# Value projection by rows, with the attention windows gathered through DRAM

## The chip, the cores and the metric

The kernel runs on one core of one Trainium2 chip. The metric is the device time of one launch in microseconds (us). A core has TensorE (PE, matrix products), VectorE (DVE), ScalarE (ACT) and GpSimd (POOL), each with its own instruction queue that is worked off in order, and DMA engines that move data between SBUF (on-chip memory, 128 partitions), PSUM (where PE writes) and DRAM. In this kernel nearly all DMAs are issued from the queue of SyncE (SP). Engines wait for each other through semaphores. A difference under 0.2% of the time is about what a measurement of this kernel can't tell from none.

## The reference, cut to what matters

The input `x` has shape (2, 128, 256, 256), all in float32. The layer is halo attention followed by a mixture of experts, each with a normalization in front and a residual add behind.

```python
qkv = einsum('bchw,oc->bohw', ln(x), W_qkv)          # 128 channels -> q, k, v of 128 each
q = 8x8 windows of q; k, v = 12x12 windows around the same places (overlapping, zero-padded)
attn = q @ k.T * SCALE + rel_pos + FIXED_MASK        # -inf where row or column offset is of the wrong parity
x = x + W_out @ (softmax(attn) @ v)
t = tokens of x
x = x + sum over the 2 best of 8 experts: gate_e * (ln(t) @ expert_w[e] + expert_b[e])
```

The fixed mask leaves, for a query, only keys whose row and column have one parity. So the image falls into four planes (row parity by column parity) that don't see each other. In one plane a window of queries is 4 by 4, and its window of keys is 6 rows by 10 columns for two neighbouring windows taken together (60 keys, `NK`).

## The kernel before, in words

The image is cut into 64 strips of 8 rows (2 images, 32 strips each), each strip into its 4 planes: 256 steps of the main loop (line 779 on), one plane of one strip each, and 7 more that finish the experts. In a plane a strip has 4 rows of 128 queries, and 6 rows of keys (`KR`), two of which it shares with its neighbours; 128 columns of queries make 16 pairs of windows (`NP`), in two halves of 8 (`HP`).

The work inside the loop is issued in the order in which it is written: `tc.manual_schedule` covers PE, DVE, ACT, POOL and SP, so what stands first in the loop's body stands first in each queue. In step n four things are interleaved:

- attention of plane n: `scores` (L448 and L465, products of 32x64 tiles), the exponential L473 on ACT, `attend` (L486 sums, L496 values), normalization by DVE (L506 to L516), `out_project` (L524 on PE, L529 on DVE);
- the projections of plane n+1: `project`, a generator that the loop advances five times. It makes the values in two parts (`values`, L369 on PE and L376 on ACT), the relative position terms `pu` (L384, then L386, L349 and L354 on DVE), the keys `pk` (L396, copied by ACT L407 and L414 into the windowed layout `kcol`) and the queries `pq` (L418, L420);
- the experts of a row pair: `Experts.times` multiplies by the gate (L677, six times on DVE, twice on POOL), `product` is L686 on PE, eight per step, `end` is L692 on DVE;
- the normalization and routing of the next row pairs: statistics by PE (L554), `rstd` (L228 to L235 on DVE, with two activations L232 and L233 on ACT between), `route` (L587 to L619), `spread` (L625), which sends gates and the reciprocal deviations through a small DRAM tile `gd` and back, spread over all partitions: one load `rb` for the attention's normalization (L637), used by POOL's L272 in the same step to make a row of `xn`, and nine loads `sb` and `gb` (L666, L661) for the experts, used one step later.

[...] `columns` (L331) therefore has POOL copy the rows of `xn` that are new in a strip into `xcol`, window by window, and `values` then multiplies 16 blocks of two windows' keys: 8 products of 128x128 a step, `vv` with keys on the partitions. Keys of a block are ordered by ring row (`place`, a row's place modulo 6), then by column. The rows of keys that a strip shares with the one before stay in `xcol` and `kcol`, which are rings.

PSUM tiles of `mm_tile` come from one pool of three buffers in turn; a product that takes a buffer waits until the reader of the tile three before it is done. In a step that order is `pvv`, `pu`, `pk`, `pq`, `plt`, `plg`, `pvv`, `po`.

Of the kernel before, what the change touches and what calls it, by code (L numbers as in the profile page):

```python
# [11 lines left out]
F32 = mybir.dt.float32  # L12
AF = mybir.ActivationFunctionType
ALU = mybir.AluOpType
# [3 lines left out]
P = 128  # L18
# [33 lines left out]
def kernel(  # L52
# [42 lines left out]
    def ctile(shape, name):  # L95
        return const.tile(shape, F32, tag=name, name=name)
# [101 lines left out]
    xn, xcol, kcol = [], [], []  # L198
    for i in range(2):
        xn.append(ctile([P, 2, 2, KR, PC + 2], f"xn{i}"))  # L200
        nc.gpsimd.memset(xn[i][:, :, :, :, 0 : PC + 2 : PC + 1], 0.0)
    for i in range(4):
        xcol.append(ctile([P, HP, 2, SLOT], f"xcol{i}"))
        kcol.append(ctile([P, NP, SLOT], f"kcol{i}"))
        nc.gpsimd.memset(xcol[i][:, :, :, NK:], 0.0)
        nc.gpsimd.memset(kcol[i][:, :, NK:], 0.0)
        nc.gpsimd.memset(kcol[i][:, 0, 0:NK:KC], 0.0)
        nc.gpsimd.memset(kcol[i][:, NP - 1, KC - 1 : NK : KC], 0.0)


    auT = []
# [6 lines left out]
    def rstd(p4, k0, k1, name):  # L218

        u, r = (
            small.tile([P, 2, NT], F32, tag=v, name=f"{v}_{name}")[:, k0:k1] for v in ("u", "r")
        )
        mean, sq = (
            p4[:, :, E + 2 * k0 + j : E + 2 * k1 : 2].rearrange("p t k -> p k t") for j in range(2)
        )
        nc.vector.tensor_copy(r, mean)  # L228
        nc.vector.tensor_tensor(u, r, r, ALU.mult)
        nc.vector.scalar_tensor_tensor(u, u, -1.0, sq, ALU.mult, ALU.add)  # L230
        nc.vector.scalar_tensor_tensor(u, u, 0.0, epsc[:, k0:k1], ALU.max, ALU.add)
        nc.scalar.activation(r, u, AF.Ln, scale=4.0)  # L232
        nc.scalar.activation(r, r, AF.Exp, scale=-0.5)  # L233
        nc.vector.scalar_tensor_tensor(u, u, -4.0, r, ALU.mult, ALU.mult)
# [16 lines left out]
    def place(i, k):  # L251

        return (PR * strips[i][1] + k) % KR
# [69 lines left out]
            ln1(i, k, pb, nc.vector)  # L323
        yield

    def columns(n):

        i, pl = divmod(n, 4)
        for k, at, m in runs(i, ln_rows(i)):
            for half in range(2):  # L330
                nc.gpsimd.tensor_copy(  # L331
                    xcol[pl][:, :, half, at * KC : (at + m) * KC].rearrange(
                        "p t (r c) -> p t r c", c=KC
                    ),
                    windows(xn[i % 2][:, pl // 2, pl % 2, k : k + m], half * HP, HP),
                )
        for k, s in ((0, 0), (KR - 1, NS - 1)):
            if strips[i][1] == s:
                c0 = place(i, k) * KC
                nc.gpsimd.memset(xcol[pl][:, :, :, c0 : c0 + KC], 0.0)  # L340
                nc.gpsimd.memset(kcol[pl][:, :, c0 : c0 + KC], 0.0)

    def shift(uT, n, state):

# [12 lines left out]
    def project(n, state):  # L357

        i, pl = divmod(n, 4)
        xp = xn[i % 2][:, pl // 2, pl % 2]  # L360
        inner = xp[:, 1 : 1 + PR, 1 : PC + 1]
        xl, kk = xcol[pl], kcol[pl]

        vv = work.tile([P, HP, P], F32, tag="vv", name=f"vv{n}")

        def values(t0):
            pv = mm_tile(f"pvv{n}_{t0}")
            for t in range(4):
                nc.tensor.matmul(  # L369
                    pv[:, t * P : (t + 1) * P],  # L370
                    lhsT=xl[:, t0 + t].rearrange("p a k -> p (a k)"),
                    rhs=wv,
                    start=True,
                    stop=True,
                )
            nc.scalar.copy(vv[:, t0 : t0 + 4, :].rearrange("p t c -> p (t c)"), pv)  # L376

        values(0)
        yield

        pu = mm_tile(f"pu{n}")
        nc.tensor.matmul(pu, lhsT=wrel, rhs=inner, start=True, stop=True)  # L384
        uT = work.tile([P, PR, 4, 32], F32, tag="uT", name=f"uT{n}", bufs=1)
        nc.vector.transpose(uT, pu.rearrange("p (a m s) -> p a s m", a=PR, s=4))  # L386
        state["shift"] = lambda: shift(uT, n, state)
        yield

        rows = list(ln_rows(i))  # L390
        for part in (rows[-4:], rows[:-4]):
            if not part:
                continue
            pk = mm_tile(f"pk{n}_{part[0]}")
            m = len(part)
            nc.tensor.matmul(  # L396
                pk[:, : m * PC],
                lhsT=wk,
                rhs=xp[:, part[0] : part[0] + m, 1 : PC + 1],
                start=True,  # L400
                stop=True,
            )
            pk3 = pk[:, : m * PC].rearrange("p (r c) -> p r c", r=m)
            for k, at, m in runs(i, part):
                new = pk3[:, k - part[0] : k - part[0] + m]
                places = kk[:, :, at * KC : (at + m) * KC].rearrange("p t (r c) -> p t r c", c=KC)
# [3 lines left out]
                for j, step in enumerate(((NP - 1) * SLOT - 1, PC - KC + 1)):  # L410
# [12 lines left out]
        yield  # L423

        values(4)
        state.update(qs=qs, kk=kk, vv=vv)
        yield

    def windows(rows, n0, count):
# [192 lines left out]
    def spread(f, c, g, nm):  # L622

        gT = small.tile([P, 2, 32], F32, tag="gT", name=f"gT{nm}")
        nc.vector.transpose(  # L625
            gT.rearrange("p k i -> p (k i)"), g.rearrange("p k b j -> p (k b j)")
        )
        gd = dram.tile([2 * E * NT, P], F32, tag="gd", name=f"gd{nm}")

        to = gd.rearrange("(k j t) (b i) -> k (t b) j i", k=2, j=E, i=32)  # L630
        for k in (1, 0):
            if k or f:
                nc.sync.dma_start(to[k], gT[:, k])
        rb = None
        if c:
            rb = gates.tile([P, NT * P], F32, tag="rb", name=f"rb{nm}", bufs=2)
            nc.sync.dma_start(rb, to_all(gd, E + 1))  # L637
        return gd, rb

    def to_all(gd, j):  # L640

# [103 lines left out]
            next(part)  # L745
    if len(strips) > 1:
        halo(1)
    columns(0)
    states = {0: {}}
    for _ in project(0, states[0]):  # L750
        pass
    states[0]["shift"]()
    if n_planes > 1:
        columns(1)

# [22 lines left out]
    with tc.manual_schedule(engines={ET.PE, ET.DVE, ET.Activation, ET.Pool, ET.SP}):  # L778
        for n in range(n_planes + 7):
# [89 lines left out]
def shape_constants():  # L869

    keys = np.zeros((HEADS, 32, 3, 2, KR, KC), np.float32)
    for turn in range(3):
        for r in range(KR):
            keys[:, r, turn, :, (r + 2 * turn) % KR, :] = 1.0
    for w in range(2):
        for c in range(KC):
            keys[:, KR + c - 4 * w if 0 <= c - 4 * w < 6 else KR + 6, :, w, :, c] = 1.0
    keys = np.pad(keys.reshape(P, 3, 2, NK), ((0, 0), (0, 0), (0, 0), (0, SLOT - NK)))
# [47 lines left out]
```

The softmax here doesn't subtract the row's maximum and nothing guards it: scores larger than these inputs give would overflow.

## Time and profile before

| what | value |
|---|---|
| median of 3 runs | 4483.97 us (4482.62 to 4489.09) |
| profiled execution, span | 4480.1 us |
| PE busy | 4422.6 us (99%) |
| DVE busy | 3996.2 us (89%) |
| ACT busy | 1467.7 us (33%) |
| POOL busy | 1317.7 us (29%) |
| DMA engines, share of the span, SP's queue | 58.3%, 813.46 MB |
| granted TensorE clock, mean | 0.997 |

The profiled execution is one launch of its own; its span, from the first to the last instruction, is 3.9 us under the median of the runs. A step of the loop takes 17.17 us in the trace in the mean of the long middle part. PE's records overlap[...]; the time that a product takes from PE is therefore read from start to start, not from its own length. A float32 product shows as two matmul records. "Idle before" in a group's line is time in which that engine did nothing just ahead of those instructions.

### The profile page before, as it was taken

The numbers are of one execution on the slowest core, as the hardware profiler recorded it, in microseconds if no ns is written. First come the engines' busy times: TensorE is split into PE (matmuls) and PEld (weight loads), VectorE is DVE, ScalarE is ACT, GpSimd is POOL, SyncE is SP. The second block draws the span as 40 slices with busy tenths as digits, with TensorE's granted clock in tenths as the row PEclk, the third lists the DMA queues.
The fourth block names the chain that finished last, engine by engine and source line by source line (L and its number), as shares of the span: only waits on it lengthen the run. The fifth ranks groups of instructions, "written<-read, shape, count | busy, mean of one in ns | idle before, by whom it ended". The sixth has DMA issues, their size and how long they took to land. (4 is left out here: it accounts for less than half of the span.)

```text
span 4480.1 us, 224632 instructions
## 1 busy us (share of the span) xinstructions
PE 4422.6 (99%) x96321; PEld 2683.3 (60%) x96321; DVE 3996.2 (89%) x11850; ACT 1467.7 (33%) x4022; POOL 1317.7 (29%) x1815
## 2 busy tenths in 40 slices
PE   7999999999999999999999999999999999999997
PEld 5666666666666666666666666666666666666653
DVE  5899999999899999998989999999999999989887
ACT  3333333333333333333333333333333333333321
POOL 1232323232323233232323232323232323232321
PEclk9999999999999999999999999999999999999999
DMA  2565666566656666666666566666665666566655
GB/s 83 174 191 185 192 185 192 186 191 185 193 184 192 185 191 187 189 188 188 189 187 189 187 190 185 193 183 193 184 193 185 192 185 192 186 191 186 190 164 186
DMA packets 519284, 828.12 MB, mean 185 GB/s; under 512 B 124186, under 2 KB 125850, under 8 KB 518298
## 3 DMA queue, kind: packets, MB, share of 16 engines
q1 hardware_dynamic: 517568, 813.46, 58.3%
q8 instruction: 769, 12.60, 1.1%
q14 instruction: 217, 1.78, 0.2%
q10 hardware_dynamic: 730, 0.29, 0.0%
HBM read 737.95 MB, written 75.56 MB: 182 GB/s over the span
## 5 line engine op out<-in xcount | busy, mean ns | idle before, releaser
L686 PE MATMUL acc<-xe,ew 128*128 128x512 f32 x4096 | 1889.0, 594 | 19.6 <-DVE gb L660 18.8
L686 PEld LDWEIGHTS acc<-xe,ew 128*128 128x128 f32 x4096 | 758.8, 190 | 885.7 <-issue 861.8
L677 DVE TENSOR_TENSOR xe<-xs,gb 128x512 f32<-128x512 f32 x1536 | 950.9, 687 | 10.2 <-PE acc L686 0.7
L681 POOL COPY last<-xe 128x1 f32<-128x1 f32 x256 | 47.9, 187 | 3060.8 <-DVE gb L660 3054.6
L376 ACT COPY vv<-pvv 128x512 f32<-128x512 f32 x512 | 299.8, 586 | 1395.7 <-PE pvv L369 1379.6
L677 POOL TENSOR_TENSOR xe<-xs,gb 128x512 f32<-128x512 f32 x512 | 650.8, 1272 | 5.9 <-PE att L496 2.5
L369 PE MATMUL pvv<-wt,xcol 128*128 128x128 f32 x4096 | 594.3, 288 | 2.5 <-POOL xcol L331 1.5
L369 PEld LDWEIGHTS pvv<-wt,xcol 128*128 128x128 f32 x4096 | 496.4, 191 | 64.8 <-issue 51.8
L272 POOL TENSOR_TENSOR xn<-xt,rb 128x512 f32<-128x512 f32 x249 | 375.0, 1506 | 66.5 <-DMA rb<-gd 55.9
L465 PE MATMUL att<-qs,kcol 32*64 32x32 f32 x32768 | 392.4, 226 | 0.8 <-issue 0.7
L465 PEld LDWEIGHTS att<-qs,kcol 32*64 32x64 f32 x32768 | 391.0, 130 | 1.0 <-issue 1.0
L496 PEld LDWEIGHTS att<-pT,vv 64*32 64x32 f32 x32768 | 348.0, 105 | 39.4 <-issue 2.5
L496 PE MATMUL att<-pT,vv 64*32 64x32 f32 x32768 | 343.2, 200 | 2.3 <-issue 2.3
L473 ACT ACTIVATE pT<-att 128x1024 f32<-128x1024 f32 x256 | 261.9, 1023 | 243.1 <-PE att L465 239.7
L548 ACT ACTIVATE sq<-xt 128x512 f32<-128x512 f32 x505 | 292.7, 631 | 0.0
L354 DVE STREAM_TRANSPOSE au<-auT 128x512 f32<-128x512 f32 x256 | 269.2, 1052 | 9.0
L524 PE MATMUL po<-o,wt 128*128 128x512 f32 x512 | 262.0, 593 | 6.1 <-DVE o L516 3.2
L384 PE MATMUL pu<-xn,wrel 128*128 128x512 f32 x512 | 262.5, 594 | 0.0
L407 ACT COPY kcol<-pk 128x560 f32<-128x560 f32 (+2 forms) x344 | 174.1, 506 | 268.2 <-PE pk L396 265.3
L418 PE MATMUL pq<-xn,wt 128*128 128x512 f32 x512 | 262.0, 593 | 0.0
L396 PE MATMUL pk<-xn,wt 128*128 128x512 f32 (+2 forms) x528 | 261.0, 578 | 0.0
L386 DVE STREAM_TRANSPOSE uT<-pu 128x512 f32<-128x512 f32 x256 | 182.8, 714 | 78.0 <-PE pu L384 77.0
(2697 smaller groups left out, 5243.8 us busy)
## 6 DMA issues: line engine op xcount, KB each, us to landing
gb<-gd SPq DMA_DIRECT2D x2048, 256.0 KB, 4.0
xt<-in_x_dram SPq DMA_DIRECT2D x256, 256.0 KB, 4.9
sb<-gd SPq DMA_DIRECT2D x256, 256.0 KB, 3.5
out_dram<-xt SPq DMA_DIRECT2D x256, 256.0 KB, 4.2
rb<-gd SPq DMA_DIRECT2D x249, 256.0 KB, 3.3
gd<-gT SPq DMA_DIRECT2D x516, 16.0 KB, 3.0
ew<-in_L_ffn_expert_w_dram SPq DMA_DIRECT2D x1, 512.0 KB, 5.0
eb<-in_L_ffn_expert_b_dram SPq DMA_DIRECT2D x1, 512.0 KB, 5.7
```

The source lines that it names most:

```text
L272: eng.tensor_tensor(xn[i % 2][:, :, :, k, 1 : PC + 1], ln1_src(i, k).rearrange("p (y j x) -> p y x j", y=2, x=2), rb.rearrange("p (y j x) ...
L354: nc.vector.transpose(au.rearrange("p m a s -> p a s m"), auT[n % 2])
L369: nc.tensor.matmul(pv[:, t * P : (t + 1) * P], lhsT=xl[:, t0 + t].rearrange("p a k -> p (a k)"), rhs=wv, start=True, stop=True,)
L376: nc.scalar.copy(vv[:, t0 : t0 + 4, :].rearrange("p t c -> p (t c)"), pv)
L384: nc.tensor.matmul(pu, lhsT=wrel, rhs=inner, start=True, stop=True)
L418: nc.tensor.matmul(pq, lhsT=wq, rhs=inner, start=True, stop=True)
L465: nc.tensor.matmul(sc[rows, h, 32 * t : 32 * t + 32], lhsT=kk[hp, half * HP + t, :], rhs=qs[hp, m0 : m0 + 2].rearrange("p m a s -> p (m a ...
L496: nc.tensor.matmul(av[hp, half, 32 * t : 32 * t + 32], lhsT=vv[rows, t, hp], rhs=pT[rows, h, 32 * t : 32 * t + 32], start=True, stop=True,)
L524: nc.tensor.matmul(po, lhsT=wo, rhs=state["o"].rearrange("p f z -> p (f z)"), start=True, stop=True)
L548: nc.scalar.activation(sq, src, AF.Square)
L677: eng.tensor_tensor(self.xe[e], self.xs, self.gb.pop(e), ALU.mult)
L686: nc.tensor.matmul(self.acc, lhsT=ew[:, e, :], rhs=self.xe.pop(e), start=(e == 0), stop=not self.xe)
```

## The change

- The values are no longer computed from windowed blocks. `value_rows` multiplies each new row of a plane by the value weights: a row's 128 columns are the stationary operand, so the product has columns on the partitions and the 128 value channels along the free dimension. For most strips that is 4 products of 128x128 a step into one PSUM tile, and one ACT copy into `vr`; strips at an image's top and bottom have 5 and 3 rows.
- `send_values` stores `vr` in DRAM, in a ring `vrows` for each plane, by column and then by ring row: one store of 256 KB, two where the new rows wrap around the ring (one strip in three).
- `take_values` loads the windows from there: two loads a step, one for each half of the windows, of 60 keys by 8 windows by 512 bytes, into `vwin`, which takes the place of `vv`.
- A block's keys are now ordered by column, then by ring row, in `kcol` (L434 and L441 on ACT) and in the constant `c_keys` too.
- `xcol` and POOL's copies into it are gone; `borders` keeps the clearing of rows outside the image.
- In the loop, `send_values` stands between the stores of `gd` and the load of `rb`; `take_values` stands behind the load of `sb`, ahead of the first `gb`. `project` now begins with `pu`, then the value products, and its fifth part issues nothing.
- In `rstd`, the square is now taken as r times `mean`, where `mean` is still the PSUM tile, and not as r times r.

```diff
-        nc.vector.tensor_tensor(u, r, r, ALU.mult)
+        nc.vector.tensor_tensor(u, r, mean, ALU.mult)
...
-    def columns(n):
+    def borders(n):
...
+    def value_rows(n):
+        i, pl = divmod(n, 4)
+        xp = xn[i % 2][:, pl // 2, pl % 2]
+        rows, sent = list(ln_rows(i)), []
+        for part in (rows[-4:], rows[:-4]):
...
+            pv = mm_tile(f"pv{n}_{part[0]}")
+            for j, k in enumerate(part):
+                nc.tensor.matmul(
+                    pv[:, j * P : (j + 1) * P],
+                    lhsT=xp[:, k, 1 : PC + 1],
+                    rhs=wv,
...
+            vr = work.tile([P, 4, P], F32, tag="vr", name=f"vr{n}_{part[0]}")
+            nc.scalar.copy(
+                vr[:, 0:m].rearrange("p r c -> p (r c)"), pv[:, : m * P]
+            )
...
+    def send_values(n, sent):
+        i, pl = divmod(n, 4)
+        for part, vr in sent:
+            for k, at, m in runs(i, part):
+                nc.sync.dma_start(
+                    vrows[pl][1 : PC + 1, at : at + m, :],
+                    vr[:, k - part[0] : k - part[0] + m],
+                )
+
+    def take_values(n):
+        for half in range(2):
+            src = vrows[n % 4][half * HP * 8 : half * HP * 8 + KC].rearrange("c r d -> (c r) d")
+            src = src.unsqueeze(1)
+            dims = [list(d) for d in src.ap]
+            dims[1] = [8 * KR * P, HP]
+            nc.sync.dma_start(
+                vwin[n % 2][half * SLOT : half * SLOT + NK],
+                bass.AP(src.tensor, src.offset, dims),
+            )
...
-        values(0)
-        yield
...
         nc.tensor.matmul(pu, lhsT=wrel, rhs=inner, start=True, stop=True)
+        state["sent"] = value_rows(n)
+        yield
+
...
-        values(4)
-        state.update(qs=qs, kk=kk, vv=vv)
+        state.update(qs=qs, kk=kk, vv=vwin[n % 2])
         yield
...
-                gd, rb1 = spread(f, c, made[0], f"_{n}")
-                row = (*c, rb1) if c else None
+                gd = spread(f, c, made[0], f"_{n}")
                 new = Experts(*f, gd) if f else new
+            if n + 1 < n_planes:
+                send_values(n + 1, states[n + 1]["sent"])
+            if gated and c:
+                row = (*c, fetch_rstd(gd, f"_{n}"))
             next(ahead, None)
...
             new.fetch_means()
+            if n + 1 < n_planes:
+                take_values(n + 1)
...
             if n + 2 < n_planes:
-                columns(n + 2)
+                borders(n + 2)
```

More of the change, by code (lines that the diff above doesn't have):

```diff
@@ L196 @@
     nc.vector.tensor_copy(wrel, pr[:, :P])
-    xn, xcol, kcol = [], [], []
+    xn, vwin, vrows, kcol = [], [], [], []
+    zero = ctile([P, KR, P], "zero")
+    nc.gpsimd.memset(zero, 0.0)
     for i in range(2):
+        vwin.append(ctile([P, HP, P], f"vwin{i}"))
+        nc.gpsimd.memset(vwin[i], 0.0)
         xn.append(ctile([P, 2, 2, KR, PC + 2], f"xn{i}"))
@@ L202 @@
     for i in range(4):
-        xcol.append(ctile([P, HP, 2, SLOT], f"xcol{i}"))
         kcol.append(ctile([P, NP, SLOT], f"kcol{i}"))
-        nc.gpsimd.memset(xcol[i][:, :, :, NK:], 0.0)
+        vrows.append(dram.tile([PC + 2, KR, P], F32, tag=f"vrows{i}", name=f"vrows{i}", bufs=1))
+        nc.sync.dma_start(vrows[i][0 : PC + 2 : PC + 1], zero[0:2])
         nc.gpsimd.memset(kcol[i][:, :, NK:], 0.0)
-        nc.gpsimd.memset(kcol[i][:, 0, 0:NK:KC], 0.0)
-        nc.gpsimd.memset(kcol[i][:, NP - 1, KC - 1 : NK : KC], 0.0)
+        nc.gpsimd.memset(kcol[i][:, 0, 0:KR], 0.0)
+        nc.gpsimd.memset(kcol[i][:, NP - 1, NK - KR : NK], 0.0)
     auT = []
@@ L324, in first_norms @@
         yield
-    def columns(n):
+    def borders(n):
         i, pl = divmod(n, 4)
[L329 to L336, printed above, removed]
         for k, s in ((0, 0), (KR - 1, NS - 1)):
@@ L338, in columns @@
             if strips[i][1] == s:
-                c0 = place(i, k) * KC
-                nc.gpsimd.memset(xcol[pl][:, :, :, c0 : c0 + KC], 0.0)
-                nc.gpsimd.memset(kcol[pl][:, :, c0 : c0 + KC], 0.0)
+                at = place(i, k)
+                nc.gpsimd.memset(kcol[pl][:, :, at:NK:KR], 0.0)
+                nc.sync.dma_start(vrows[pl][1 : PC + 1, at, :], zero[:, 0, :])
+    def value_rows(n):
[3 more added lines that the diff above has]
+        for part in (rows[-4:], rows[:-4]):
+            if not part:
+                continue
+            pv = mm_tile(f"pv{n}_{part[0]}")
+            m = len(part)
+            for j, k in enumerate(part):
[3 more added lines that the diff above has]
+                    rhs=wv,
+                    start=True,
+                    stop=True,
+                )
[3 more added lines that the diff above has]
+            )
+            sent.append((part, vr))
+        return sent
@@ new lines, in send_values @@
+    def send_values(n, sent):
[15 more added lines that the diff above has]
+                bass.AP(src.tensor, src.offset, dims),
+            )
@@ L361, in project @@
         inner = xp[:, 1 : 1 + PR, 1 : PC + 1]
[L362 to L376, printed above, removed]
-        values(0)
-        yield
+        kk = kcol[pl]
         pu = mm_tile(f"pu{n}")
         nc.tensor.matmul(pu, lhsT=wrel, rhs=inner, start=True, stop=True)
+        state["sent"] = value_rows(n)
+        yield
         uT = work.tile([P, PR, 4, 32], F32, tag="uT", name=f"uT{n}", bufs=1)
@@ L405, in project @@
                 new = pk3[:, k - part[0] : k - part[0] + m]
-                places = kk[:, :, at * KC : (at + m) * KC].rearrange("p t (r c) -> p t r c", c=KC)
+                places = kk[:, :, 0:NK].rearrange("p t (c r) -> p t r c", r=KR)[:, :, at : at + m]
                 nc.scalar.copy(places[:, 1 : NP - 1], windows(new[:, :, KC - 3 :], 0, NP - 2))
                 ends = [places[:, 0, :, 1:], new[:, :, 0 : KC - 1]]
-                for j, step in enumerate(((NP - 1) * SLOT - 1, PC - KC + 1)):
+                for j, step in enumerate(((NP - 1) * SLOT - KR, PC - KC + 1)):
                     dims = [list(d) for d in ends[j].unsqueeze(1).ap]
@@ L633, in spread, with fetch_rstd @@
                 nc.sync.dma_start(to[k], gT[:, k])
[L634 to L638, printed above, removed]
+        return gd
+    def fetch_rstd(gd, nm):
+        rb = gates.tile([P, NT * P], F32, tag="rb", name=f"rb{nm}", bufs=2)
+        nc.sync.dma_start(rb, to_all(gd, E + 1))
+        return rb
     def to_all(gd, j):
@@ L747 @@
         halo(1)
-    columns(0)
+    borders(0)
     states = {0: {}}
@@ L752 @@
     states[0]["shift"]()
+    send_values(0, states[0]["sent"])
+    take_values(0)
     if n_planes > 1:
-        columns(1)
+        borders(1)
     onesm = ctile([P, P], "onesm")
@@ L877, in shape_constants @@
             keys[:, KR + c - 4 * w if 0 <= c - 4 * w < 6 else KR + 6, :, w, :, c] = 1.0
+    keys = keys.swapaxes(-1, -2)
     keys = np.pad(keys.reshape(P, 3, 2, NK), ((0, 0), (0, 0), (0, 0), (0, SLOT - NK)))
```

## The prediction

> **What bounds the kernel now.** First the page's busy times and the costliest groups.
>
> ```profile
> span 4480.1 us, 224632 instructions
> PE 4422.6 (99%) x96321; PEld 2683.3 (60%) x96321; DVE 3996.2 (89%) x11850; ACT 1467.7 (33%) x4022; POOL 1317.7 (29%) x1815
> L369 PE MATMUL pvv<-wt,xcol 128*128 128x128 f32 x4096 | 594.3, 288 | 2.5 <-POOL xcol L331 1.5
> ```
>
> PE is full, and between 145 and 4300 us it is busy for 4154.93 of 4155 us. VectorE has 89%, but that leaves little: I therefore looked at what its idle time is. The chain of waits on the page covers only the last 25 us, so I took one step from the timeline instead (PE, VectorE and GpSimd asked apart).
>
> ```profile
> 2089.33 1.16 PE L369 MATMUL pvv<-wt,xcol 128*128 128x128 f32 x8
> 2090.32 1.02 PE L384 MATMUL pu<-xn,wrel 128*128 128x512 f32 x2
> ...
> 2084.15 0.83 DVE L229 TENSOR_TENSOR u__120_39077<-r__120_39078 128x8 f32<-128x8 f32 x1
> 2085.01 0.16 DVE L230 SCALAR_TENSOR_TENSOR u__120_39077<-u__120_39077,plg 128x8 f32<-128x8 f32 x1
> 2085.21 0.17 DVE L231 SCALAR_TENSOR_TENSOR u__120_39077<-u__120_39077,epsc 128x8 f32<-128x8 f32 x1
> 2085.89 0.17 DVE L234 SCALAR_TENSOR_TENSOR u__120_39077<-u__120_39077,r__120_39078 128x8 f32<-128x8 f32 x1 [0.52 <-ACT r__120_39078 L233]
> ...
> 2082.23 1.51 POOL L272 TENSOR_TENSOR xn<-xt,rb 128x512 f32<-128x512 f32 x1
> 2083.69 1.26 POOL L677 TENSOR_TENSOR xe<-xs,gb 128x512 f32<-128x512 f32 x1
> 2084.90 0.84 POOL L331 COPY xcol<-xn 128x320 f32<-128x320 f32 x2
> ```
>
> Four value products hold PE for 0.99 us (2089.33 to 2090.32). L229 works on 8 elements a partition and takes 0.83 us: it ends 0.03 us after GpSimd's product L677 (2083.69 + 1.26). It is held by that instruction.
>
> VectorE's mean step in steps 36 to 235 of the trace is 17.17 us: 15.55 busy, 0.84 in gaps of about 0.034 us between dependent instructions, 0.79 in longer ones. Of the longer ones 0.48 (0.52 less a normal gap) is the trip to ScalarE behind L231, which a step always has; 0.18 is L386 waiting for `pu` (77.0 us in the list of waits), 0.04 is L529, the rest small. So VectorE alone would need some 16.9 us a step: it is a quarter of a microsecond from being the bound.
>
> [...] L230 reads PSUM and is always 0.16, and once in this trace L229 slipped through ahead of the product, and L231, with both inputs in SBUF, was held instead:
>
> ```profile
> 1998.21 0.35 DVE L229 TENSOR_TENSOR u__115_37452<-r__115_37453 128x8 f32<-128x8 f32 x1
> 1998.60 0.16 DVE L230 SCALAR_TENSOR_TENSOR u__115_37452<-u__115_37452,plg 128x8 f32<-128x8 f32 x1
> 1998.79 1.00 DVE L231 SCALAR_TENSOR_TENSOR u__115_37452<-u__115_37452,epsc 128x8 f32<-128x8 f32 x1
> ...
> 1998.50 1.27 POOL L677 TENSOR_TENSOR xe<-xs,gb 128x512 f32<-128x512 f32 x1
> ```
>
> [...]
>
> **The change part by part**
>
> *PE.* Eight value products become four. Start to start both groups cost 0.99 us (2082.00 to 2082.99 is the other), so PE's step falls from 17.17 to 16.18 us. `pu` moves ahead of the values. In the built order `pq` now takes `pu`'s PSUM buffer and waits for VectorE's L386.
>
> *VectorE, L229.* It now reads one input from PSUM and should take 0.165 us. But L231 still reads two SBUF inputs. It would be reached 0.165 + 0.034 + 0.16 + 0.034 = 0.39 us after L229's start, while GpSimd's product still runs (0.80 us from there), and end with it as in step 115, at 0.83. Before, L231 ended at 0.83 + 0.03 + 0.16 + 0.04 + 0.17 = 1.23. So 0.40 us are gained, not the 0.67 that L229 alone loses. In a third of the strips L231 now takes 0.29, held by the second pair of copies L331; without them 0.12/3 = 0.04 more. Every fourth step has the ring copy L246 (0.62) ahead of the product: there L229 takes 1.30 and the gain is 0.40 too. Sum 0.44.
>
> *VectorE, L386.* `pu` ends a microsecond earlier, so the 0.18 goes, and L529's 0.04 likewise, since `po` comes earlier.
>
> *The new bound.* VectorE's step is 17.17 - 0.44 - 0.18 - 0.04 = 16.51 us, over PE's 16.18. The loop then runs VectorE (L625 to the sixth L677), GpSimd (L681, two products, L272: 0.2 + 1.27 + 1.51 + 1.27), VectorE (L231 to the next L625), and PE waits.
>
> *PE's trip.* PE, ahead by 0.33 us a step, is stopped at `pq` by L386. In the trace a PE product starts 0.15 us after the VectorE instruction that it waits for; from `pq` to the end of L496 are 6.18 us, and L506 starts 0.11 after that: 6.44 us from L386's end, against 6.25 now. L506 would come 0.19 late. That lies beside GpSimd's 4.2 us, inside the 0.44 for which L231 is held anyway: nothing; if the hold were gone, 0.19.
>
> *GpSimd.* The copies L331 go (about 0.9 us a step), behind its last product: nothing depends on them any more.
>
> *ScalarE.* One 0.59 us copy fewer. The remaining one (`vr`) waits for value products that now end later relative to `pu`; the marker copy for `gb` 7 and, behind it on SP, `gd` wait for it. With PE ahead as above, `pv` ends 0.06 us before L625 starts, `vr` is done at 0.63, the marker at 0.8; before it was done at 0.34. So `gd` and `rb` go out about 0.45 us later. The store of `vrows` sits between them, but `rb` waits 2 us for `gd`'s landing anyway, and the issue takes 0.33. Now `rb` is issued at 2077.55, lands after 3.3 (3.0 to 3.8 in the tile's list), and L272 starts at 2082.23: 1.4 us spare. After: 1.4 - 0.45 - 0.22 (VectorE and with it GpSimd are earlier) = 0.7 spare. Cost nothing; uncovered, each 0.1 us of lateness adds 0.1 to the step.
>
> *DMA.* A step adds 128 packets of 2 KB and 960 of 512 B. In the trace's packet records 2 KB take 84 to 103 ns, 512 B (loading `ew`) 27 to 31: (128 x 0.094 + 960 x 0.029)/16 = 2.5 us an engine. Now the DMAs take 0.61 x 17.17 = 10.5 us; 13.0 of 16.5 is 79%. The window loads wait for the store (about 4.2 us, like `out_dram`) and hold SP until some 7 us into the step, so the first `gb` goes 2 us later; each `gb` is used some 10 us or more after. The windows land at about 12 us and are used at 22. Nothing.
>
> *ScalarE's key copies* now write with stride 6: unknown. Below 0 nothing can come; at double their 0.85 us they still end before L548's result is needed (PE's L554, 3.4 us of room). I take 0.
>
> *Start.* Store and load of the first plane cost about 9 us from 26 us on; its L486 ran at 39 us. I take 0; up to 5.
>
> **The sum.** 248 steps of this length: 248 x 0.66 = 164 us. Profiled span 4480.1 - 164 = 4316; the runs' median is 3.9 above the profiled one: 4320. Its own range, 4290 to 4370, takes in the start, the key copies, and L506's 0.19 counted in part (248 x 0.19 = 47).
>
> **Rivals**
>
> 1. *PE stays the bound.* If L231 isn't held, VectorE falls by a further 0.27 (0.7 in ring-copy steps) and PE's 16.18 decides: 4484 - 248 x 0.99 = 4238. For it: 99% on PE. Against: step 115.
> 2. *Partly given back.* L506's wait counts in full and `rb` comes 0.3 us late: 16.51 + 0.19 + 0.3 = 17.0, 4484 - 248 x 0.17 = 4442; half of that 4380. For it: transfers issued close together land later than `rb` does now (`gb` 4.0, `xt` 4.9).
> 3. *Slower.* `rb`, now behind a 256 KB store, takes 4.9 us like `xt`, and `gd` 0.2 longer: 1.8 late, 1.1 beyond the spare 0.7. Step 17.6, 4484 + 248 x 0.44 = 4593. It decides once `rb` lands 1.36 us (0.7 + 0.66) later than I forecast. Against: the store should be through before `rb` is issued, 1.4 us after it.
> 4. *No change*: rival 3 at just 1.36.
>
> **How the numbers follow.** The main case has 0.50, rival 1 0.14, rival 2 0.20, slower 0.12, no change (within 0.2%, about what a measurement can tell) 0.04. Faster: 0.50 + 0.14 + 0.20 = 0.84. The range from 4235 to 4425 takes in rival 1 and most of rival 2, and leaves out the last two and the upper end of rival 2, about 0.2.
>
> **What would show it.** PE near 96% busy with a wait at `pq` for L386; VectorE near 94%; L229 at 0.17 and L231 near 0.6, ending with GpSimd's L677; no idle time of GpSimd before L272 on `rb`; DMA near 0.79. GpSimd waiting for `rb` says rival 2 or 3; PE at 99% says rival 1; a wait of L522 (L496 now) for a DMA would say that the gather is late, which I exclude.

## The result, and the profile after

The changed kernel takes 4410.63 us (median of 4 runs, 4409.01 to 4415.92) against 4485.05 us before (4 runs, 4482.62 to 4489.09). The ratio is 0.9837, 95% interval 0.9823 to 0.9851. It is faster by 74 us; the forecast was 164. The profiled execution took 4415.92 us, the longest of the four.

The head of the page and the two queues that matter, after the change:

```profile
span 4414.1 us, 224656 instructions
PE 4254.2 (96%) x94273; PEld 2453.1 (56%) x94273; DVE 3844.2 (87%) x11850; ACT 1455.9 (33%) x3774; POOL 1092.5 (25%) x1126
...
q1 hardware_dynamic: 822864, 1007.52, 74.6%
q8 instruction: 769, 12.60, 1.2%
```

PE fell from 99% to 96% as forecast, but VectorE fell from 89% to 87% instead of rising to 94%. So VectorE isn't the bound, and PE, at 96%, stands still for a part of each step. The list of waits (engine, line and what it waited for; us in total, times, longest) names places that before cost little or weren't there:

```profile
POOL xn L276 <- DMA rb<-gd: 165.4, 129, 29.2
PEld pq L445 <- DVE uT L413: 162.9, 235, 2.2
DVE sT L532 <- PE att L522: 124.1, 184, 3.8
PE acc L714 <- issue: 44.9, 73, 2.2
PE att L474 <- issue: 30.7, 8, 13.3
```

The same list of the kernel before has these lines for GpSimd's wait, VectorE's wait for attention and PE's wait ahead of scores; PE's stop within the expert product (L714) has no counterpart there:

```profile
POOL xn L272 <- DMA rb<-gd: 55.9, 4, 24.7
DVE sT L506 <- PE att L496: 10.6, 10, 2.6
PE att L448 <- issue: 9.6, 8, 6.8
```

GpSimd waits for `rb` 129 times instead of 4. VectorE waits for attention 184 times instead of 10. And PE stands still for "issue", which is to say for nothing that the profile shows: 73 times in the middle of an expert product, and 8 times ahead of scores, once for 13.3 us.

**A ledger for PE.** From one `gT` (VectorE's last instruction of the routing, L651, whose result goes out through `gd`) to the next, over steps 40 to 231, a step takes 16.80 us for 17.17 before. PE's own work without any stop is 16.29 us of it. The remaining 0.51 lies almost wholly at three records of a step, found by comparing each matmul's distance to the next with its usual distance: 0.03 within L491 (record 46 of 368), 0.20 at `pq` (L445) waiting for `uT`, and 0.27 between the first and second pass of the first expert product (record 174). Records are PE's matmuls, counted from the start of scores; each comes with a weight load. In the kernel before the same three sum to 0.00. Records 46 and 174 (and 302, where nothing is lost) lie 128 records, 256 instructions, apart: PE's program is fetched in blocks of that size (the trace has 196,673 matmuls, weight loads and empty instructions on PE and 769 packets on the queue called instruction; 769 x 256 = 196,864), and `addr_align` pins the blocks to the step. This is one such stop in the timeline (start, duration, engine, line, idle time before):

```profile
1053.11 0.59 ACT L358 COPY vr<-pv 128x512 f32<-128x512 f32 x1 [0.93 <-PE pv L350]
1053.59 0.20 ACT L686 COPY gb<-onesm 128x1 f32<-128x1 f32 x1
1053.78 1.13 PE L445 MATMUL pq<-xn,wt 128*128 128x512 f32 x2
1053.82 0.32 SPq L689 DMA_DIRECT2D gb<-gd  x1
1054.23 1.58 SPq L659 DMA_DIRECT2D gd<-gT  x2
1054.75 0.59 PE L714 MATMUL acc<-xe,ew 128*128 128x512 f32 x1
1055.86 0.58 SPq L369 DMA_DIRECT2D vrows<-vr  x1
1056.22 1.02 PE L714 MATMUL acc<-xe,ew 128*128 128x512 f32 x2 [0.88 <-issue]
```

Two things are to be seen. PE's first pass starts at 1054.75 and its second, of the same product with inputs that have long been there, only at 1056.22. And on ScalarE the marker copy for `gb` 7 (L686) stands behind the value copy `vr` (L358); SyncE issues that `gb` and then `gd` only after it.

In the trace's packet records each block arrives as one packet of 16 KB on that queue. Means over the steps, in us:

| block that begins at record | kernel | fetch starts after the block before it began | fetch ends before its own block begins | PE's stop |
|---|---|---|---|---|
| 174 | before | 2.39 | 1.57 | 0.00 |
| 174 | after | 3.22 | 0.96 | 0.27 |
| 46 | before | 2.00 | 4.26 | 0.00 |
| 46 | after | 2.41 | 2.82 | 0.03 |

In the changed kernel's single steps PE doesn't stop at record 174 where the fetch ended at least about 1 us before; it stops 0.25 us where the fetch ended 0.75 us before, and 0.43 where it ended 0.55 before.

The `rb` chain in the same steps: the second `gd` transfer is issued 2.00 us after `gT`'s start (1.29 before), `rb` at 4.82 (3.80) and it lands at 8.32 (7.05). Part of that is the later issue (0.71); the rest is that `gd` takes 3.36 us from issue to landing for 3.11 before, and `rb` 3.48 for 3.25.

**Theories.** Mine: the missing 0.29 us a step come from a late `rb` and from late instruction fetches, and some 20 us from the two ends of the program. The rival: PE's trip from `uT` through `pq` and attention back to VectorE's L532 is a fixed loop that bounds the kernel, and transfers are only seen to wait.

### The profile page after: what moved, and what is told of

Same layout as the page of the kernel before. It is cut to its first block, busy times and chain, and to the rows that moved or that the text cites. A ratio compares the mean times of both kernels' runs of the same rounds, so it can differ in the third digit from the quotient of the medians.

```text
span 4414.1 us, 224656 instructions
## 1 busy us (share of the span) xinstructions
PE 4254.2 (96%) x94273; PEld 2453.1 (56%) x94273; DVE 3844.2 (87%) x11850; ACT 1455.9 (33%) x3774; POOL 1092.5 (25%) x1126
## 3 DMA queue, kind: packets, MB, share of 16 engines
q8 instruction: 769, 12.60, 1.2%
## 5 line engine op out<-in xcount | busy, mean ns | idle before, releaser
L714 PE MATMUL acc<-xe,ew 128*128 128x512 f32 x4096 | 1935.8, 602 | 66.7 <-issue 44.9
L714 PEld LDWEIGHTS acc<-xe,ew 128*128 128x128 f32 x4096 | 759.2, 190 | 1001.6 <-issue 931.2
L705 DVE TENSOR_TENSOR xe<-xs,gb 128x512 f32<-128x512 f32 x1536 | 951.0, 687 | 12.3 <-DMA gb<-gd 2.2
L705 POOL TENSOR_TENSOR xe<-xs,gb 128x512 f32<-128x512 f32 x512 | 650.8, 1272 | 2.5 <-PE acc L714 1.6
L276 POOL TENSOR_TENSOR xn<-xt,rb 128x512 f32<-128x512 f32 x249 | 374.0, 1502 | 171.5 <-DMA rb<-gd 165.4
L491 PE MATMUL att<-qs,kcol 32*64 32x32 f32 x32768 | 396.9, 226 | 4.8 <-issue 4.7
L491 PEld LDWEIGHTS att<-qs,kcol 32*64 32x64 f32 x32768 | 394.4, 131 | 6.3 <-issue 5.8
L522 PEld LDWEIGHTS att<-pT,vwin 64*32 64x32 f32 x32768 | 348.0, 105 | 37.5 <-issue 0.4
L522 PE MATMUL att<-pT,vwin 64*32 64x32 f32 x32768 | 343.3, 200 | 0.2 <-issue 0.2
L350 PEld LDWEIGHTS pv<-wt,xn 128*128 128x128 f32 x2048 | 270.5, 192 | 127.4 <-issue 80.1
L434 ACT COPY kcol<-pk 128x560 f32<-128x560 f32 (+2 forms) x344 | 318.9, 927 | 52.4 <-PE pk L423 49.0
L532 DVE STREAM_TRANSPOSE sT<-att 128x512 f32<-128x512 f32 x256 | 183.5, 717 | 133.4 <-PE att L522 124.1
L445 PE MATMUL pq<-xn,wt 128*128 128x512 f32 x512 | 272.8, 614 | 23.4 <-DVE uT L413 21.4
L408 PE MATMUL pu<-xn,wrel 128*128 128x512 f32 x512 | 293.0, 654 | 0.0
L350 PE MATMUL pv<-wt,xn 128*128 128x128 f32 x2048 | 271.3, 275 | 0.9 <-issue 0.9
L474 PEld LDWEIGHTS att<-au,keys 32*64 32x64 f32 x8192 | 117.2, 132 | 227.7 <-PE po L550 183.5
```

Of the source, the lines that this page charges most:

```text
L276: eng.tensor_tensor(xn[i % 2][:, :, :, k, 1 : PC + 1], ln1_src(i, k).rearrange("p (y j x) -> p y x j", y=2, x=2), rb.rearrange("p (y j x) ...
L350: nc.tensor.matmul(pv[:, j * P : (j + 1) * P], lhsT=xp[:, k, 1 : PC + 1], rhs=wv, start=True, stop=True,)
L491: nc.tensor.matmul(sc[rows, h, 32 * t : 32 * t + 32], lhsT=kk[hp, half * HP + t, :], rhs=qs[hp, m0 : m0 + 2].rearrange("p m a s -> p (m a ...
L522: nc.tensor.matmul(av[hp, half, 32 * t : 32 * t + 32], lhsT=vv[rows, t, hp], rhs=pT[rows, h, 32 * t : 32 * t + 32], start=True, stop=True,)
L705: eng.tensor_tensor(self.xe[e], self.xs, self.gb.pop(e), ALU.mult)
L714: nc.tensor.matmul(self.acc, lhsT=ew[:, e, :], rhs=self.xe.pop(e), start=(e == 0), stop=not self.xe)
```

## The experiments

All are timed against the kernel before, 4485 to 4487 us in each batch; where not said otherwise they are edits of the changed kernel.

**1. The marker of `gb` 7 ahead of the value copy.** `fetch` writes one column of the buffer, the marker, which SyncE waits for before it issues the load; `gd` stands behind that load in SyncE's queue.

```diff
             next(score, None)
-            next(ahead, None)
             nxt.fetch(7, nc.scalar)
+            next(ahead, None)
```

> The changed kernel (4411 us) with one statement moved: ScalarE meets the wait that guards the gd transfer before it copies the values of the next row, not after. Transfer theory (GpSimd's L276 waits 0.39 us a step for rb, half of it because gd is issued 0.7 us later behind the value copy; a kernel bound by late transfers): gd is issued about 0.7 us earlier, the wait falls to about 0.15 a step, 0.25 x 245 = 60 us, about 4350 us. Rival (PE's trip from uT through pq and attend to L532 is the bound, transfers are cover): 4405 to 4411, the wait of L276 only changes place with another.

4372.37 us, ratio 0.9752 (0.9735 to 0.9770): 38 us less than the changed kernel, 60 had been expected. The wait for `rb`:

```profile
POOL xn L276 <- DMA rb<-gd: 90.1, 20, 31.8
```

20 times for 129; in the steady steps 0.03 us for 0.39. `rb` lands at 7.36. PE's wait at `pq` fell with it, from 0.20 to 0.04 a step, so that wait came from `rb`: as I read it, a late L276 holds back GpSimd's last products and with them VectorE. The fixed-loop rival falls here. But the fetch stops stayed, 0.32 for 0.31: the one at record 174 fell to 0.11 and the one at record 46 rose to 0.21. The 60 had counted GpSimd's wait; PE had only its 0.20 at `pq` to gain from it, and 0.16 x 248 = 40 us is what came.

**2. No value transfers in the loop.**

```diff
-                send_values(n + 1, states[n + 1]["sent"])
...
-                take_values(n + 1)
```

> The changed kernel without any transfer of value rows within the loop: neither the stores to DRAM nor the loads of vwin. It leaves out that computation: attention multiplies with the values of the prologue in every plane. Transfer theory: rb, xt and the PE's instruction fetch are on time again, a step of about 16.3 for 16.8, about 4411 - 0.45 x 245 = 4300 us; PE's stalls in the first expert product and VectorE's wait for attend shrink. Rival (the engines' own loop is the bound): within 10 us of 4405.

4376.49 us, ratio 0.9747 (0.9731 to 0.9763). This missed both numbers. The fetch stops fell to 0.14 a step, as my theory says. The other half of it fell:

```profile
POOL xn L276 <- DMA rb<-gd: 161.6, 121, 26.3
PEld pq L445 <- DVE uT L413: 179.5, 235, 2.6
```

`rb` is as late as ever without any value traffic: it lands 8.43 us after `gT`'s start. Its lateness comes of the order on ScalarE, not of the value transfers; I had put half of it down to them. The order works in two ways: in experiment 1 `gd` goes out at 1.17, 0.83 earlier, and also takes only 2.83 us to land (3.36 in the changed kernel, 3.70 here). Why its own transfer is quicker there isn't shown. And the value traffic isn't the whole cause of the fetch stops: 0.14 us are left without it, most of it at record 46, whose fetch starts 3.52 us after the block before it began (2.41 in the changed kernel).

**3. Both together.**

> The edit that puts the gd transfer's guard ahead of the value copy and the removal of all value transfers together (it leaves out the computation of values in attention: vwin stays that of the prologue). Alone they gave 4372 and 4376. Two-cause theory (a late rb comes of the order on ScalarE, late instruction fetches come of the value transfers; each hides behind the other in a loop): wait for rb below 0.05 us a step, fetch stalls about 0.14, PE's wait at pq below 0.05, a step of 16.35 to 16.45, 4305 to 4325. Rival (one common cause, or the engines' own loop at 16.65): 4365 to 4375.

4308.58 us, ratio 0.9606 (0.9592 to 0.9621). Both causes are gone:

```profile
POOL xn L276 <- DMA rb<-gd: 62.7, 4, 27.5
```

The steady wait for `rb` is 0.00, that at `pq` 0.05, the fetch stops are 0.05, and a step takes 16.39. Together the two edits are worth 102 us, more than 38 + 34 alone: taking one cause away leaves the other, and part of the gain reappears there (the stop at record 46 in experiment 1, the wait at `pq` of 0.27 in experiment 2).

**4. The blocks moved by one pass.**

```diff
-BLOCK, FIRST_LIMIT = 256, 95
+BLOCK, FIRST_LIMIT = 256, 97
```

> The changed kernel with one number changed: the blocks of 256 PE instructions begin 97 instructions after the start of scores instead of 95. In the changed kernel PE stands still between the first and second pass of the first expert product (L714, record 174 of the step) for 0.27 us a step on average, where such a block begins and its 16 KB instruction fetch ends only 0.96 us before (1.57 before the change). The later start gives this fetch one pass (0.43 us) more. Fetch theory: the stall falls from 0.27 to about 0.11 a step, the next block's (record 302) rises from 0.00 to less than 0.03, and as this stall lies in the trip uT, pq, attend, L532 it shows in the step: 0.1 to 0.13 x 245, about 4380 to 4387. Rival (PE waits there for something else than its instructions): the stall stays 0.27 and stays at the first expert product's second pass, 4405 to 4415.

4385.28 us, ratio 0.9784 (0.9764 to 0.9805): 25 us less from one number.

```profile
PE acc L714 <- issue: 15.2, 30, 1.2
PE att L491 <- issue: 10.4, 20, 1.2
```

The stop moved from record 174 to record 175, that is with the block, and fell from 0.27 to 0.09 (expected 0.11). At record 303 0.03 appeared, at record 47 the stop is 0.08 (0.03 at record 46 in the changed kernel), and the wait at `pq` is 0.24. PE stops where its block begins, not at an operand.

**5. The kernel before with the new traffic,** of a dummy tile that nothing uses.

> The kernel before with the changed kernel's value transfers added at the same places, stores of a dummy tile to DRAM and loads from it, with nothing using them: computation as before, and PE busy for the whole step of 17.17. Fetch theory: the instruction fetch before record 174 starts 0.5 to 0.9 us later than in the kernel before, PE stands still 0.1 to 0.3 us a step at the blocks' beginnings, and as PE is the bound, 4510 to 4560. Rival (PE's stalls belong to the new projection or the new order of keys): no stall, 4480 to 4490.

4719.98 us, ratio 1.0528 (1.0511 to 1.0544): far more than I expected, by the mechanism that I expected. PE's waits:

```profile
PE acc L720 <- issue: 170.4, 218, 1.9
```

L720 is the first expert product here. The stop at record 174 is 0.88 us a step: the fetch starts 3.87 us after the block before it (2.39 without the traffic) and ends only 0.10 before its own block begins. 0.88 x 248 = 218 of the 235 us. VectorE's L540, behind attention, waits 0.79 a step. The transfers aren't quite at the same places: the stores stand behind the load of `rb` here and ahead of it in the changed kernel, so they go out at 5.5 us (2.6), and the loads, which wait for them, 9.3 to 9.7 us into the step (6.8 to 7.2), closer ahead of that block's fetch. I take this to be why it costs three times as much, but no run separates it; I had not asked when they leave.

**6. L229 alone,** in the kernel before: `tensor_tensor(u, r, mean)` for `(u, r, r)`.

> The kernel before (4485 us) with only its L229 changed: the square is taken of one SBUF tile and the PSUM mean (r by mean) as in the changed kernel, so that this instruction isn't held by GpSimd (0.93 us before, 0.17 after); projection, values and all transfers stay as before. The forecast's VectorE sum without PE's relief: PE is busy for 17.17 of 17.17 us a step, so 4475 to 4485, no change. If L229 alone carries the gain whatever PE does: about 4485 - 0.4 x 248 = 4385.

4481.46 us, ratio 0.9989 (0.9982 to 0.9995). Where PE is busy all the time, 0.73 us less on VectorE's L229 are worth 0.1%. The timeline of the step that the prediction used shows the hold go where it said:

```profile
2084.70 1.27 POOL L677 TENSOR_TENSOR xe<-xs,gb 128x512 f32<-128x512 f32 x1
2085.17 0.16 DVE L229 TENSOR_TENSOR u__120_39077<-r__120_39078,plg 128x8 f32<-128x8 f32 x1
2085.36 0.16 DVE L230 SCALAR_TENSOR_TENSOR u__120_39077<-u__120_39077,plg 128x8 f32<-128x8 f32 x1
2085.56 0.43 DVE L231 SCALAR_TENSOR_TENSOR u__120_39077<-u__120_39077,epsc 128x8 f32<-128x8 f32 x1
```

L231, with two inputs in SBUF, ends at 2085.99, with GpSimd's product (2084.70 + 1.27 = 2085.97). Its mean is 0.54 us here, 0.23 before.

**7. No hold at all.**

```diff
-        nc.vector.scalar_tensor_tensor(u, u, -1.0, sq, ALU.mult, ALU.add)
-        nc.vector.scalar_tensor_tensor(u, u, 0.0, epsc[:, k0:k1], ALU.max, ALU.add)
+        for k in range(k0, k1):
+            eps = (FFN_EPS, CONV_EPS)[k]
+            nc.vector.scalar_tensor_tensor(
+                u[:, k - k0], sq[:, k - k0], eps, u[:, k - k0], ALU.add, ALU.subtract)
```

> The changed kernel with the two VectorE instructions of rstd that read two (or one) SBUF tiles (L234, L235) replaced by one instruction per kind which adds eps and subtracts (the clamp of the variance at zero is left out). It frees VectorE from the hold of GpSimd's L677, which after the change lies on L235 (0.373 us a step for 0.219 before). If the hold is what VectorE's chain lost: up to 0.2 us a step, 4360 to 4375. Transfer theory: the time saved on VectorE is lost again in the waits for rb and for PE, 4395 to 4411.

4398.58 us, ratio 0.9809 (0.9794 to 0.9823), within my theory's range. PE waits less at `pq` (0.11 for 0.20), but GpSimd waits more for `rb` (0.66 for 0.39) and the fetch stops rise to 0.38. What VectorE gains it waits for elsewhere.

**8. Short pads.**

```diff
-                nc.tensor.addr_align(BLOCK, offset=BLOCK - FIRST_LIMIT)
+                nc.tensor.addr_align(BLOCK, offset=BLOCK - FIRST_LIMIT, max_nops=40)
```

> The changed kernel with the padding of PE's program ahead of scores limited to 40 empty instructions in a row (longer ones are jumped). The changed kernel has 205 of them before the first aligned step and 67 before each of the last four, with PE idle 13.3 us there (6.75 before the change) and 2.4 to 2.8 (0.5) before each of the last four. Padding theory: the start gains up to 10 us and the end up to 8: 4393 to 4402, steady step unchanged at 16.80. Rival (other work waits there anyway): 4408 to 4412.

4385.00 us (4372.68 to 4406.84), ratio 0.9767 (0.9751 to 0.9784): 26 us less, somewhat over what I expected. Scores of the first aligned step, in the timeline of PE, of the changed kernel and then of this one:

```profile
122.34 1.16 PE L474 MATMUL att<-au,keys 32*64 32x128 f32 x32 [13.34 <-issue]
...
139.84 0.70 PE L474 MATMUL att<-au,keys 32*64 32x128 f32 x32 [1.57 <-issue]
```

```profile
111.49 1.14 PE L474 MATMUL att<-au,keys 32*64 32x128 f32 x32 [0.81 <-PE po L550]
...
132.69 0.69 PE L474 MATMUL att<-au,keys 32*64 32x128 f32 x32
```

In its trace the eighth `gT` comes 154.7 us after the start (163.1 in the changed kernel, 152.8 before), and from the 251st to VectorE's last product it takes 154.4 us (166.3, and 154.2 before). The steady step is 16.83. So of the changed kernel's losses at both ends, 10.4 and 12.1 us, 8.5 and 11.9 were empty instructions. There are 205 of them before the first aligned step; 193 of these stand in one row in the trace and take 14.35 us, 74 ns each.

**9. The three cheap edits together** (1, 4 and 8).

> Three edits together on the changed kernel: the gd transfer's guard ahead of the value copy (alone -38 us), blocks of PE instructions from instruction 97 (alone -25), pads of at most 40 empty instructions (alone -26). If each cause has its own share: with the guard moved, the stall at the first expert product was only 0.11 a step, so the block start gives 0.08 x 245 = 20; 4411 - 38 - 20 - 25, about 4330, 4320 to 4340. If they hide each other as in a loop with one bound: 4355 to 4372.

4331.04 us (4325.73 to 4340.72), ratio 0.9657 (0.9639 to 0.9675). This beats both kernels, and each cause keeps its own share, as the first theory said. A step is 16.54.

```profile
span 4324.0 us, 224271 instructions
PE 4229.6 (98%) x94273; PEld 2462.2 (57%) x94273; DVE 3799.2 (88%) x11850; ACT 1457.7 (34%) x3774; POOL 1087.0 (25%) x1126
```

What is left is the stop at the block within L491 (record 47), 0.18 a step.

**10. The three edits, and the window loads at other places.** After the load of the input rows:

```diff
-            if n + 1 < n_planes:
-                take_values(n + 1)
...
             load_x((n + 9) // 4, (n + 9) % 4, paced=True)
+            if n + 1 < n_planes:
+                take_values(n + 1)
```

> The three edits, and the loads of vwin issued after the load of the next input rows instead of ahead of the first gates' (SyncE waits 162 us for the stores of the values at the old place). Fetch theory: gb and xt leave earlier and the fetch that is requested at record 303 (about 7.2 us into the step) finds fewer vwin packets ahead of it, its stall of about 0.2 a step falls to 0.1, while that at record 175 may rise by as much: within 20 us of the three edits, either way. If the place of the loads doesn't matter for PE's stalls: both stalls as in the three edits within 0.03 a step.

4466.83 us, ratio 0.9961 (0.9948 to 0.9974): 136 us more than the three edits, where I had said within 20. Both stops grew, to 0.44 at record 47 and 0.33 at record 175:

```profile
PE att L491 <- issue: 84.4, 94, 5.5
PE acc L714 <- issue: 53.6, 103, 1.1
```

At the old place the loads leave at 5.8 and 6.3 us. Now two `gb`, the rows, both loads and another `gb` leave between 6.7 and 9.5 us into the step, and everything behind them lands later: the loads after 7.7 and 8.2 us, the output rows after 7.3 (5.8 in experiment 1). The fetches start 4.18 and 4.07 us after their block began, 3.47 and 3.25 with the three edits.

As the last transfers of the step instead (after `new.fetch(6, dve)`):

> The three edits, and the loads of vwin issued as the last transfers of the step. Fetch theory: the fetch for record 175, requested about 13.7 us into the step, then stands behind vwin's packets as well, its start 0.5 to 1 us later; stall there 0.4 to 0.8 a step for about 0.03, and the next step's gd and rb late too: 4410 to 4500. If transfers only matter by their sum and not by when they are issued: as the three edits within 10 us.

4527.20 us, ratio 1.0099 (1.0081 to 1.0117), slower than the kernel before and beyond the 4410 to 4500 expected. Not for the reason given first: the fetch for record 175 starts no later than with the three edits (3.24 us after the block before it began, 3.25 there), and the stop is 0.25, under the 0.4 to 0.8 expected; another 0.26 stands at record 47. Here `gd` is issued behind the loads and lands 5.45 us after its issue (3.37 in experiment 1), and GpSimd waits for `rb` 1.13 us a step, PE at `pq` 0.44.

```profile
POOL xn L276 <- DMA rb<-gd: 342.9, 235, 31.5
```

**11. The three edits and no hold.**

> The three edits, and rstd without the instruction that GpSimd's L677 holds (L234 and L235 as one instruction per kind, the clamp of the variance at zero left out). PE's work with the fetch stalls that are left is about 16.5 a step, so if PE is the bound now: 0 to -8 us against the three edits. If VectorE's chain still is: up to 0.2 x 245 = 50 us less.

4320.78 us (4311.72 to 4333.69), ratio 0.9634 (0.9613 to 0.9655). That is 10 us less than the three edits, where 0 to 8 had been expected, but the ranges of the runs overlap, and the steady step is the same 16.54: with transfers in order, PE and its fetches are the bound and VectorE's hold costs next to nothing.

**The ledger over all of them.** 16.29 us of PE's work plus the stops gives the step within 0.04 in every edit of the changed kernel:

| kernel | stops at block starts | wait at `pq` | sum | step measured |
|---|---|---|---|---|
| changed | 0.31 | 0.20 | 16.80 | 16.80 |
| 1 marker first | 0.32 | 0.04 | 16.65 | 16.65 |
| 2 no value traffic | 0.14 | 0.27 | 16.70 | 16.69 |
| 3 both | 0.05 | 0.05 | 16.39 | 16.39 |
| 4 block start 97 | 0.20 | 0.24 | 16.73 | 16.72 |
| 7 no hold | 0.38 | 0.11 | 16.78 | 16.77 |
| 8 short pads | 0.33 | 0.21 | 16.83 | 16.83 |
| 9 three edits | 0.22 | 0.03 | 16.54 | 16.54 |
| 10 loads after rows | 0.77 | 0.01 | 17.07 | 17.11 |
| 10 loads last | 0.58 | 0.44 | 17.31 | 17.34 |
| 11 three edits, no hold | 0.25 | 0.00 | 16.54 | 16.54 |

The base is taken from the first row; the others test that PE stands still nowhere else. The table is bookkeeping: it says where PE stands still, and the experiments say why. The steps are those of the profiled executions, which in experiments 1, 2, 4, 7 and 8 took 9 to 22 us longer than the median of the runs, so that they give the medians only roughly.

## Why the prediction was right or wrong

The direction was right, but the gain was 74 us for the 164 forecast: 4411 lies outside the main case's own 4290 to 4370, and only in the wide range that takes in the rivals. 0.29 us a step are missing (16.80 for 16.51), 0.29 x 248 = 72 us, and about 22 at the two ends; together 94, and the profiled execution differs from the forecast's span by 98. Two steps failed that the prediction had put at nothing, ScalarE's later `gd` and the added DMA traffic: they show as 0.20 us a step of waiting at `pq` and as 0.31 us of fetch stops. Two sizes were off as well, VectorE's sum, which made it the bound, and PE's relief.

*"VectorE, L229": the mechanism right, a size off.* It takes 0.162 us for 0.90, and its successor is held in its place (experiment 6). The trace of before shows the hold in single executions: 249 of the 260 of L229 took over 0.25 us, and 246 of these ended 0.02 to 0.03 us after one of GpSimd's L677. In the changed kernel this instruction (L233) took 0.157 to 0.165 us all 260 times. L235 (L231 before) was held less than said, 0.37 for about 0.6: 116 of its 260 executions took over 0.25 us, 97 of them ending 0.02 to 0.03 us after GpSimd's L705. In the steady steps the two instructions together fell from 1.15 to 0.53, by 0.62 for the 0.44 forecast. Why it is held less stays open.

*"The new bound": wrong.* VectorE's 16.51 was not the bound. With the 0.62 in place of 0.44 the same sum gives 16.33 (an estimate), close to PE's 16.29. Experiment 3 ran at 16.39, with VectorE still waiting 0.25 us of it at L532, and experiment 11 took the hold away for nothing in the step. PE's own step decided, with its stops counted.

*"PE": the mechanism right, a size off.* Eight value products became four, but PE's relief is 0.88, not 0.99. A value group was 0.997 us, of which its first pass took 0.213 and the others 0.11; that extra goes with the place behind another kind of product and stays there when the group is gone. Now the first pass of `pu` takes 0.534 for 0.432 and the first of L714 behind L580 0.533 for 0.432. 2 x 0.997 - 0.890 - 0.102 - 0.101 = 0.90. I subtracted a group's whole length.

*"ScalarE": this step failed.* "0.45 later", "0.7 spare", "cost nothing": the second `gd` went out 0.71 later, `rb` 1.02 later, and it landed 1.27 later. The spare was overrun in about half of the steps. The step had the right chain (value copy, marker, `gd`, `rb`) and priced it too low: the issue came 0.26 later than it said, and the 0.5 us more that `gd` and `rb` took to land weren't in it. Experiments 1 and 3 show that the place of the copy ahead of the marker did it, experiment 2 that the value transfers did not.

*"DMA": this step failed.* The share was right, 0.77 in the steady part for 0.79, and the windows were in time: no wait of L522 for a transfer shows. The "nothing" was wrong, because what the added packets could delay was asked for `gb` and the windows and not for PE's own program. The trace of before showed it: packets on the instruction queue, and a fetch that ended 1.57 us before its block. PE began to stop in the changed kernel at about 1 us, so that margin was some 0.6 us from costing something (an estimate from these two).

*"PE's trip … nothing": a size off.* From the end of `uT` to L532 (L506 before) the trip took 6.88 us for 6.27, 0.61 longer for the 0.19 that I had worked out. 0.27 of it is the stop at record 174, which lies inside it; but in experiment 3, with almost no stops, it still took 6.64. VectorE waits 0.44 us a step at L532, and since PE is the bound, that wait by itself cost nothing that the runs show.

*"Start … I take 0; up to 5": wrong.* 10 us were lost at the start and 12 at the end, nearly all of them to pads (experiment 8); the change altered the number of instructions ahead of the alignment, and 205 empty instructions stand before the first aligned step for 104 before.

*Rivals.* Rival 2, partly given back, 4380 to 4442, is the one whose range came true: GpSimd waiting for `rb` was named as its sign. It held 0.20. It was right in part by luck: it named a late `rb`, for which it pointed to transfers issued close together (experiment 2 refutes that for the value transfers), and it knew nothing of the fetches, the larger share of the loss. Rival 1's 4238 is PE's 16.18 without stops; the best here, 4309 with part of the work left out, doesn't reach it. Rival 3 needed `rb` 1.36 later than forecast; it came 1.27 later than before, which is 0.82 later than forecast, and the kernel did not become slower.

## What to carry to other kernels

When a change adds DMA traffic to a kernel whose PE is nearly full, ask for PE's own program too: look in the packet records how long before its block each instruction fetch ends, and ask which of the new transfers will be under way when the fetch is due: in these runs the time at which they left changed the stops as much as their number did (experiments 2, 5 and 10). Here a copy ahead of a marker on the same engine sent `gd`, which is issued behind that marker's load, 0.83 us later (experiment 1): put the marker first. And where a program is padded to a block, count the pads again after any change in the number of instructions (205 for 104 here).

## What the runs showed of the hardware

- PE's instruction blocks of 256 come as packets of 16 KB on the DMA queue called instruction (769 of them, 12.60 MB, in either trace). In the traces a fetch starts, on average, 1.1 to 4.2 us after PE enters the block before, and takes 0.9 to 1.2 us. For record 174 it started 2.39 us after in the kernel before, 3.22 in the changed kernel, and 3.87 where the loads left just ahead of it (experiment 5). PE stopped at record 174 where the fetch ended less than about 1 us before that record, which is 1.4 us before record 175, the one that is held back; counted to the record that is held back, the stops at record 47 in experiments 9 and 10 begin at the same 1.4 us. The stops at the blocks' beginnings sum to 0.00 us a step in the kernel before and 0.31 in the changed kernel; in experiment 5 the one at record 174 is 0.88.
- The block from record 46 to 174 lasts 4.9 us before and 5.2 after, and so does the one from 174 to 302. Only the first led to a stop of any size (0.27 for 0.00): the fetch in it starts 2.39 and 3.22 us in, in the other 1.15 and 2.09. With the blocks equally long, what differs between them is mainly when the fetch starts.
- An empty PE instruction took about 74 ns (193 in a row, 14.35 us). 31 of them in each steady step show no gap ahead of scores; 205 at once show 13.34 us.
- ScalarE's key copy of 128x560, which now writes with a stride of 6 elements, takes 1192 ns for 625 before, nearly the double that the prediction allowed for; no wait for its result stands out in the lists.
- How long the window loads took from issue to landing changed with the time at which they left: 4.4 to 5.4 us in experiment 1, 7.7 to 8.2 a few microseconds later in the step (the first place of experiment 10).
